# A CIN kernel: the contraction of 819 rows packed into six passes of 128 rows and one of 64 rows on two row tiles of TensorE

## Chip, cores and metric

One core of one Trainium2 chip. Times are device microseconds (us) of one execution; I quote the median of three or four, with the lowest and highest. Spans and everything else in a profile come from one profiled execution, which reads about 2 us shorter than its time. A run is told "slow" when it is over 1.5% above the fastest of the same kernel; ratios use fast runs only. Where kernels have slow runs among theirs, I compare their ratios to the kernel before: a difference of ratios times 860 us, the time of the kernel before.

## The reference

A compressed interaction network over x of shape (B, F, E) = (1024, 39, 64), fp32, with three layers of 64 outputs each and a final dot product:

```python
def _cin_layer(Xk, X0, W, b):
    Wr = W.reshape(O, Hk, Fdim)
    return jnp.einsum('bhe,bfe,ohf->boe', Xk, X0, Wr) + b[None, :, None]
Xk = X0
for W, b in ((W0, b0), (W1, b1), (W2, b2)):
    Xk = _cin_layer(Xk, X0, W, b)
    outs.append(Xk.sum(axis=-1))
return jnp.concatenate(outs, axis=-1) @ fc_w.T + fc_b
```

The kernel folds layers 2 and 3 into weights at the start. What is left per (b, e) is a contraction over the symmetric products x_i x_j, which with 39 linear rows are 819 rows, against 128 columns of weights.

## The kernel before

The batch is cut into 32 blocks of 2048 columns (32 samples of 64). Per block, x is loaded with one field per partition (`load`), stored twice below itself in DRAM (`store`), and copied back from there in rotated row orders (`roll`), so that the product of two copies yields 117 different pairs. Seven such products of 117 rows are made by VectorE and contracted by TensorE:

```python
def load(n, engine):                       # one transfer, issued by GpSimd
    engine.dma_start(xs[n]..., xv[:, n * BB : (n + 1) * BB, :])

def store(n):                              # 2 x 312 KB
    nc.sync.dma_start(xd[n][0:F], xs[n])
    nc.sync.dma_start(xd[n][F:FW], xs[n])

def roll(n):                               # 4 x 936 KB + 2 x 312 KB
    for i in range(4):
        nc.sync.dma_start(r[n][i], rows(xd[n], BASE[i], [(1, F), (STEP[i], NG)], BLK))
    nc.sync.dma_start(qt[0:K:NG], xd[n][LAST : LAST + F])
    nc.sync.dma_start(qt[1:K:NG], xd[n][0:F])
# ... cut: weights ...
def product(n, c):
    a, b = (r[n][PAIRS[c][0]], r[n][PAIRS[c][1]]) if c < len(PAIRS) else (r[n][0], q[n % 2])
    nc.vector.tensor_tensor(p, a, b, ALU.mult)          # 117 x 2048

def multiply(n, c, p):
    for m in range(BLK // MM):                          # 4 column groups of 512
        nc.tensor.matmul(po[n][m // 2][...], wa[:, c, :], p[:, bass.ts(m, MM)], ...)
# ... cut ...
for at, (n, c) in enumerate(steps):                     # 7 chunks a block
    if c == 0:
        roll(n + 1); store(n + 2); load(n + 3, nc.gpsimd)
    multiply(n, c, p.pop((n, c)))
    if c == 0:
        finish(n - 1); fields(n)
    p[steps[at + 4]] = product(*steps[at + 4])
```

One turn of the SP queue is thus: six copies for block n+1, then the store of block n+2. There are two sets of copies.

Of the kernel before, what the change touches and what calls it, by code (L numbers as in the profile page):

```python
# [33 lines left out]
F32 = mybir.dt.float32  # L37
AF = mybir.ActivationFunctionType
ALU = mybir.AluOpType
AX = mybir.AxisListType  # L40

B, F, E, H = 1024, 39, 64, 64
FH = F * H
NG = 3
K = NG * F
STEP = (0, 15, 9, 6)
BASE = (0, 3, 5, 20)
LAST = 11
PAIRS = ((0, 1), (0, 2), (1, 2), (0, 3), (1, 3), (2, 3))
NCHUNK = len(PAIRS) + 1  # L50
MM = 512
SUB = 1024
BLK = 2048
# [3 lines left out]
FW = 2 * F  # L57
# [3 lines left out]
    min(d % F, -d % F)  # L61
    for i, k in PAIRS
    for j in range(NG)
    for d in [(STEP[k] - STEP[i]) * j + BASE[k] - BASE[i]]
)
assert sorted(_dist + [LAST]) == list(range(1, F // 2 + 1))
assert max(2 * s + b for s, b in zip(STEP, BASE)) < F


def rows(t, first, steps, n):  # L70

    base = t[:]
    width = base.ap[-1][1] if len(base.ap) == 2 else n
    ap = [[s * width, k] for s, k in steps] + [[1, n]]
    return bass.AP(base.tensor, base.offset + first * width, ap)
# [3 lines left out]
def cin_kernel(ctx: ExitStack, tc: tile.TileContext, x, w0t, b0, w1, b1, w2, b2, fc_w, fc_b, out):  # L79
    nc = tc.nc  # L80
# [3 lines left out]
    const = ctx.enter_context(tc.tile_pool(name="const", bufs=1))  # L84
    dram = ctx.enter_context(tc.tile_pool(name="dram", bufs=1, space=DRAM))
    xds = ctx.enter_context(tc.tile_pool(name="xds", bufs=5, space=DRAM))
    stage = ctx.enter_context(tc.tile_pool(name="stage", bufs=4))
    rolls = ctx.enter_context(tc.tile_pool(name="rolls", bufs=2))
    prods = ctx.enter_context(tc.tile_pool(name="prods", bufs=4))
    psum = ctx.enter_context(tc.tile_pool(name="psum", bufs=4, space=PSUM))  # L90
    ctx.enter_context(tc.manual_schedule())

    xv = x.rearrange("b f e -> f b e")
    xs, xd, r = {}, {}, {}
# [10 lines left out]
        nc.sync.dma_start(xd[n][F:FW], xs[n])  # L105

    def roll(n):
        r[n] = [rolls.tile([K, BLK], F32, name=f"r{i}", tag=f"r{i}") for i in range(4)]
        for i in range(4):
            nc.sync.dma_start(r[n][i], rows(xd[n], BASE[i], [(1, F), (STEP[i], NG)], BLK))  # L110
        qt = q[n % 2]
        nc.sync.dma_start(qt[0:K:NG], xd[n][LAST : LAST + F])
        nc.sync.dma_start(qt[1:K:NG], xd[n][0:F])

    wa = const.tile([K, NCHUNK, 2 * H], F32, name="wa")
    wb = const.tile([K, NCHUNK, 2 * H], F32, name="wb")
    fc = const.tile([H, 3], F32, name="fc")
    fc2 = const.tile([H, 32], F32, name="fc2")
    v2 = const.tile([H, FX], F32, name="v2")
# [3 lines left out]
    wfin = const.tile([H + F, 1], F32, name="wfin")  # L123
    kfin = const.tile([1, 1], F32, name="kfin")

    q = [const.tile([K, BLK], F32, name=f"q{i}") for i in range(2)]

    wide0 = dram.tile([FW * FW, H], F32, name="wide0")
    wide0v = wide0.rearrange("(b a) h -> b (a h)", a=FW)
    wide = dram.tile([FX * FW, H], F32, name="wide")  # L130
# [3 lines left out]
    with prep as prep:  # L134

        w2s = prep.tile([H, FH], F32, name="w2s")
        w1s = prep.tile([H, FH], F32, name="w1s")
        nc.sync.dma_start(w2s, w2)
        nc.scalar.dma_start(fc, fc_w.rearrange("o (l h) -> h (o l)", h=H))
        nc.scalar.dma_start(w1s, w1)  # L140
        load(0, nc.sync)
        w0v = w0t.rearrange("b a h -> b (a h)")
        for i in range(2):
            for k in range(2):
                engine = nc.scalar if i else nc.gpsimd
                engine.dma_start(wide0v[i * F : (i + 1) * F, k * F * H : (k + 1) * F * H], w0v)
        nc.scalar.dma_start(bias[:, 0:1], b1.rearrange("(h o) -> h o", o=1))
        nc.scalar.dma_start(bias[:, 1:2], b2.rearrange("(h o) -> h o", o=1))
        nc.scalar.dma_start(b0s[H:128], b0.rearrange("(h o) -> h o", o=1))
        nc.scalar.dma_start(fcb, fc_b.rearrange("(p o) -> p o", o=1))  # L150
        for qt in q:
            nc.gpsimd.memset(qt, 1.0)  # L152
        store(0)
        roll(0)

        nc.vector.memset(wa[:, NCHUNK - 1, :], 0.0)
        nc.vector.memset(wb[:, NCHUNK - 1, :], 0.0)
        nc.vector.memset(wfin[0:H], 1.0)
        nc.vector.tensor_copy(fc2, fc[:, 2:3].to_broadcast([H, 32]))  # L159
        nc.vector.tensor_copy(v2[:, FW:FX], fc[:, 1:2].to_broadcast([H, 2]))  # L160


        n8 = 8 * F
        pv = psum.tile([128, 2, MM], F32, name="pv", tag="po")
        vrow = prep.tile([128, 2, n8], F32, name="vrow")
        for half in range(2):
            for t in range(4):
                g = 4 * half + t
                nc.tensor.matmul(  # L169
                    pv[32 * t : 32 * t + 32, half, 0:n8],  # L170
                    fc2,
                    w2s[:, g * n8 : (g + 1) * n8],
                    start=True,
                    stop=True,
                )
            nc.vector.tensor_copy(vrow[:, half], pv[:, half, 0:n8])  # L176
            nc.scalar.dma_start(v2[32 * half : 32 * half + 32, 0:F], vrow[0:128:32, half])
        nc.vector.tensor_copy(v2[:, F:FW], v2[:, 0:F])  # L178


        w1v = w1s.rearrange("o (h f) -> o f h", f=F)
        for g in range(5):
            f0, f1 = 8 * g, min(8 * g + 8, F)
            n = (f1 - f0) * H
            pt = psum.tile([128, SUB], F32, name="pt", tag="po")
            nc.tensor.matmul(pt[0:FX, :n], v2, w1v[:, f0:f1, :], start=True, stop=True)  # L186
            part = prep.tile([FX, MM], F32, name=f"part{g}")
            nc.vector.tensor_copy(part[:, :n], pt[0:FX, :n])  # L188
            for k in range(2):
                nc.scalar.dma_start(widev[:, (k * F + f0) * H : (k * F + f1) * H], part[:, :n])  # L190


    def gather(engine, dst, table, i, k, cols):

        first = BASE[k] * FW + BASE[i]
        steps = [(FW + 1, F), (STEP[k] * FW + STEP[i], NG)]
        engine.dma_start(dst[:, cols], rows(table, first, steps, H))  # L197

    def line(engine, dst, table, j, cols, first, step):
        engine.dma_start(dst[j:K:NG, NCHUNK - 1, cols], rows(table, first, [(step, F)], H))  # L200

    def gathers(engine, other, table, cols):
        for c, (i, k) in enumerate(PAIRS):
            gather(engine, wa[:, c], table, i, k, cols)
            gather(engine if c < 4 else other, wb[:, c], table, k, i, cols)
        line(engine, wa, table, 0, cols, LAST * FW, FW + 1)
        line(other, wb, table, 0, cols, LAST, FW + 1)
        line(engine, wa, table, 1, cols, 0, FW + 1)

    gathers(nc.gpsimd, nc.gpsimd, wide0, slice(H, 2 * H))  # L210
    load(1, nc.gpsimd)
    load(2, nc.gpsimd)
    gathers(nc.scalar, nc.sync, wide, slice(0, H))
    line(nc.sync, wa, wide, 2, slice(0, H), FW * FW, 1)
    store(1)


# [9 lines left out]
    po, g = {}, {}  # L227

    def product(n, c):
        a, b = (r[n][PAIRS[c][0]], r[n][PAIRS[c][1]]) if c < len(PAIRS) else (r[n][0], q[n % 2])  # L230
        p = prods.tile([K, BLK], F32, name="p", tag="p")
        nc.vector.tensor_tensor(p, a, b, ALU.mult)  # L232
        return p

    def multiply(n, c, p):
        if c == 0:
            po[n] = [psum.tile([128, SUB], F32, name="po", tag="po") for _ in range(BLK // SUB)]
        for m in range(BLK // MM):
            nc.tensor.matmul(  # L239
                po[n][m // 2][:, bass.ts(m % 2, MM)],  # L240
                wa[:, c, :],
                p[:, bass.ts(m, MM)],
                start=(c == 0),
                stop=(c == NCHUNK - 1),
            )

    def fields(n):
        g[n] = []
        for h in range(BLK // SUB):
            gt = work.tile([H + F, SUB], F32, name="g", tag="g")  # L250
            nc.scalar.copy(gt[H : H + F], xs[n][:, bass.ts(h, SUB)])  # L251
            g[n].append(gt)

    def finish(n):
# [15 lines left out]
    AHEAD = 4  # L270
    steps = [(n, c) for n in range(NBLK) for c in range(NCHUNK)]
    p = {s: product(*s) for s in steps[:AHEAD]}
    for at, (n, c) in enumerate(steps):
        if c == 0:
            if n + 1 < NBLK:
                roll(n + 1)
            if n + 2 < NBLK:
                store(n + 2)
            if n + 3 < NBLK:
                load(n + 3, nc.gpsimd)  # L280
        if n == 0:
            nc.vector.tensor_tensor(wa[:, c], wa[:, c], wb[:, c], ALU.add)  # L282
        multiply(n, c, p.pop((n, c)))
        if c == 0:
            if n > 0:
                finish(n - 1)
            fields(n)
        if at + AHEAD < len(steps):
            p[steps[at + AHEAD]] = product(*steps[at + AHEAD])
# [50 lines left out]
```

## Time and profile before

| | before |
|---|---|
| time, median of 4 runs | 861.1 us (858.1 to 863.2) |
| profiled span | 856.9 us |
| TensorE busy, one block in the steady stage | 24.03 us |
| moved by the SP queue (q1) per block: copies and store | 4992 KB in 8 transfers |

Four lines of the page of the kernel before: the span, the busy tenths of TensorE and of the 16 DMA engines in 40 slices, and the DMA queue of SP (packets, MB, and the time its packets took as a share of 16 engines' span).

```profile
span 856.9 us, 5040 instructions
...
PE   1446799999999999999999999999999999999996
...
DMA  6957645767666666665766666755776666565500
...
q1 hardware_dynamic: 25003, 164.63, 54.9%
```

TensorE is full in every slice after the start; the DMA engines are never full over a slice. A measure comes from the last line: 54.9% of 16 x 856.9 us, divided by 164.63 MB, is **45.7 us of engine time per MB**. A larger figure means that the same bytes keep the engines occupied for longer.

### The profile page before, as it was taken

Reading aid. Unit: us, or ns where it says so; the run is one execution under the profiler, and the core shown is the slowest. Engines: PE = TensorE matmul, PEld = TensorE weight load, DVE = VectorE, ACT = ScalarE, POOL = GpSimd, SP = SyncE. Lnnn points to the kernel's source line nnn. Section 1 sums busy time; section 2 is a strip of 40 time slices with the busy share of each in tenths; the row PEclk is TensorE's granted clock in tenths of the full one; section 3 lists DMA queues with packets and bytes.
Section 4 is the critical chain, followed back from the end, with each engine's and each line's share of the span. In section 5 each row is a group of like instructions: output and inputs, shape, how many; then the busy total and the mean of one; then the engine's idle time right before and its main releaser. Section 6 shows DMA issues by size and latency. Waiting matters only on the chain.

```text
span 856.9 us, 5040 instructions
## 1 busy us (share of the span) xinstructions
PE 794.1 (93%) x1828; PEld 346.0 (40%) x1828; DVE 664.1 (77%) x372; ACT 140.9 (16%) x133; POOL 44.0 (5%) x54
## 2 busy tenths in 40 slices
PE   1446799999999999999999999999999999999996
PEld 0112344444444444444444444444444444444442
DVE  0333488888888888888888888888888888888883
ACT  0010121122221111122222111122222111112221
POOL 4200000000000000000000000000000000000000
PEclk9998999999999999999999999999999999999998
DMA  6957645767666666665766666755776666565500
GB/s 187 255 142 241 241 177 197 230 210 218 254 240 234 213 233 218 221 215 211 248 242 251 196 237 195 244 215 216 237 242 251 215 225 232 193 210 204 187 0 1
DMA packets 32177, 179.41 MB, mean 209 GB/s; under 512 B 8487, under 2 KB 8686, under 8 KB 11901
## 3 DMA queue, kind: packets, MB, share of 16 engines
q1 hardware_dynamic: 25003, 164.63, 54.9%
q0 software_dynamic: 4080, 11.11, 5.8%
q10 hardware_dynamic: 3070, 3.35, 1.3%
q8 instruction: 14, 0.23, 0.1%
q14 instruction: 10, 0.08, 0.0%
HBM read 156.98 MB, written 23.61 MB: 211 GB/s over the span
## 4 chain that ended last, share of the span: by engine, by line
PE 89%; DMA 7%; issue 1%; DVE 1%; ACTq 1%; SPq 0%; ACT 0%; DVEq 0%
PE po L239 89%; DMA wide<-part 2%; DMA xs<-in_x 2%; DMA r<-xd 1%; DMA v<-vrow 1%; DMA xd<-xs 1%; ACTq L197 1%; DMA wa<-wide 0%; DVE g L262 0%; DVE sums L266 0%; PE pt L186 0%; PE py L295 0%; SPq L200 0%; DVE wa L282 0%; DMA q<-xd 0%
## 5 line engine op out<-in xcount | busy, mean ns | idle before, releaser
L239 PE MATMUL po<-p,wa 117*128 117x512 f32 x1792 | 778.8, 597 | 34.6 <-DVE wa L282 34.6
L232 DVE TENSOR_TENSOR p<-r,r 117x2048 f32<-117x2048 f32 x192 | 436.8, 2289 | 142.9 <-PE po L239 132.3
L239 PEld LDWEIGHTS po<-p,wa 117*128 117x128 f32 x1792 | 342.9, 192 | 469.9 <-issue 422.4
L258 ACT ACTIVATE x<-po,b0s 64x1024 f32<-64x1024 f32 x64 | 71.1, 1112 | 495.7 <-PE po L239 495.7
L251 ACT COPY g<-xs 39x1024 f32<-39x1024 f32 x64 | 66.7, 1043 | 156.4 <-DVE sums L266 156.4
L262 DVE SCALAR_TENSOR_TENSOR g<-po,fc,x 64x1024 f32<-64x1024 f32 x64 | 81.1, 1268 | 9.8 <-ACT x L258 9.8
L266 DVE TENSOR_REDUCE sums<-g 103x16 f32<-103x1024 f32 x64 | 78.1, 1220 | 2.2
L232 DVE TENSOR_TENSOR p<-r,q 117x2048 f32<-117x2048 f32 x32 | 73.1, 2284 | 3.8 <-issue 3.8
L98 POOL DMA_DIRECT2D xs<-in_x x31 | 30.1, 975 | 680.3 <-DMA xd<-xs 397.6
L186 PE MATMUL pt<-w1s,v 64*80 64x512 f32 (+1 forms) x10 | 9.5, 1109 | 13.7 <-DVE v L178 13.7
L222 ACT ACT_TABLE_LOAD x1 | 1.3, 1283 | 57.0 <-DMA wb<-wide 57.0
L186 PEld LDWEIGHTS pt<-w1s,v 64*80 64x80 f32 x10 | 2.2, 228 | 20.4 <-DVE v L178 14.7
L178 DVE COPY v<-v 64x39 f32<-64x39 f32 x1 | 0.2, 176 | 12.9 <-DMA v<-vrow 12.9
L169 PE MATMUL pv<-w2s,fc 64*32 64x312 f32 x16 | 2.5, 724 | 7.9 <-DVE fc L159 7.3
L188 DVE COPY part<-pt 80x512 f32<-80x512 f32 (+1 forms) x5 | 3.4, 673 | 6.8 <-PE pt L186 6.8
L295 PE MATMUL py<-sums,wfin 103*1 103x512 f32 x4 | 2.9, 814 | 3.7 <-DVE sums L266 3.7
L159 DVE COPY fc<-fc 64x32 f32<-64x32 f32 x1 | 0.2, 173 | 6.0 <-DMA fc<-in_fc_w 6.0
L197 POOL DMA_DIRECT2D wa<-wide x6 | 4.1, 686 | 9.5 <-DMA wide<-in_w0t 9.0
L197 POOL DMA_DIRECT2D wb<-wide x6 | 4.3, 716 | 2.2 <-DMA wb<-wide 2.2
L169 PEld LDWEIGHTS pv<-w2s,fc 64*32 64x32 f32 x16 | 0.4, 137 | 9.0 <-DVE fc L159 7.3
L152 POOL MEMSET q<- 117x2048 f32 x2 | 3.6, 1843 | 0.0
L176 DVE COPY vrow<-pv 128x312 f32<-128x312 f32 x2 | 1.0, 482 | 2.7 <-PE pv L169 2.7
(22 smaller groups left out, 9.1 us busy)
## 6 DMA issues: line engine op xcount, KB each, us to landing
r<-xd SPq DMA_DIRECT2D x128, 936.0 KB
xd<-xs SPq DMA_DIRECT2D x64, 312.0 KB
q<-xd SPq DMA_DIRECT2D x64, 312.0 KB
xs<-in_x POOLq DMA_DIRECT2D x31, 312.0 KB, 5.2
wide<-part ACTq DMA_DIRECT2D x8, 160.0 KB
wide<-in_w0t POOLq DMA_DIRECT2D x2, 380.2 KB, 9.7
wide<-in_w0t ACTq DMA_DIRECT2D x2, 380.2 KB
w2s<-in_w SPq DMA_DIRECT2D x1, 624.0 KB
```

What stands on the lines that cost most here:

```text
L98: engine.dma_start(xs[n].rearrange("p (b e) -> p b e", e=E), xv[:, n * BB : (n + 1) * BB, :])
L152: nc.gpsimd.memset(qt, 1.0)
L169: nc.tensor.matmul(pv[32 * t : 32 * t + 32, half, 0:n8], fc2, w2s[:, g * n8 : (g + 1) * n8], start=True, stop=True,)
L186: nc.tensor.matmul(pt[0:FX, :n], v2, w1v[:, f0:f1, :], start=True, stop=True)
L188: nc.vector.tensor_copy(part[:, :n], pt[0:FX, :n])
L197: engine.dma_start(dst[:, cols], rows(table, first, steps, H))
L232: nc.vector.tensor_tensor(p, a, b, ALU.mult)
L239: nc.tensor.matmul(po[n][m // 2][:, bass.ts(m % 2, MM)], wa[:, c, :], p[:, bass.ts(m, MM)], start=(c == 0), stop=(c == NCHUNK - 1),)
L251: nc.scalar.copy(gt[H : H + F], xs[n][:, bass.ts(h, SUB)])
L258: nc.scalar.activation(t, po[n][h][H:128, :], AF.Identity, bias=b0s[H:128])
L262: nc.vector.scalar_tensor_tensor(gt[0:H], po[n][h][0:H, :], fc[:, 0:1], x1[h], ALU.add, ALU.mult)
L266: nc.vector.tensor_reduce(sums[:, b_at : b_at + SB], gt.rearrange("p (b e) -> p b e", e=E), AX.X, ALU.add)
```

## The change

The intent: 117 rows of 128 leave a part of the array unused. The 819 rows are repacked into six chunks of 128 (117 + 11 rows) and one of 64 (62 of them used). The last is laid out so that half of its columns stand on partitions 0 to 63 and the other half on 64 to 127, and the two halves go through the two row tiles of TensorE (rows 0 to 63 and 64 to 127) at the same time. That should cut a block from seven passes to six and a half. The diff, cut to its core:

```diff
 def roll(n):
-    for i in range(4):
-        nc.sync.dma_start(r[n][i], rows(xd[n], BASE[i], ...))
-    nc.sync.dma_start(qt[0:K:NG], xd[n][LAST : LAST + F])
-    nc.sync.dma_start(qt[1:K:NG], xd[n][0:F])
+    for i in range(4):
+        t = r[n][i]
+        nc.sync.dma_start(t[0:K], rows(xd[n], BASE[i], ...))
+        if i:                                      # three of 11 rows, 88 KB
+            nc.sync.dma_start(t[K:128], xd[n][EXTRA[i] : EXTRA[i] + NX])
+    for t, pieces in (                             # ten into u and v, 24 to 224 KB
+        (ut[n % 2], ((0, 56, 0), (56, 62, 28))),
+        (vt[n % 2], ((0, F, 0), (45, 56, 34), (56, 62, F))),
+    ):
+        for p0, p1, first in pieces:
+            for h in range(2):
+                nc.sync.dma_start(t[h * HR + p0 : h * HR + p1],
+                    xd[n][first : first + p1 - p0, bass.ts(h, BLK // 2)])
 def product(n, c):
+    # c < 6: p = r_i * r_k, 128 x 2048;  c == 6: h = u * v, 128 x 1024
 def multiply(n, c, p):
     for m in range(BLK // MM):
+        w, at = slice(0, 128), bass.ts(m, MM)
+        if c == NPAIR:
+            h, m = m % 2, m // 2
+            w, at = slice(h * HR, (h + 1) * HR), bass.ts(m, MM)
+            m += h * (BLK // MM // 2)
         nc.tensor.matmul(po[n][m // 2][:, bass.ts(m % 2, MM)],
-            wa[:, c, :], p[:, bass.ts(m, MM)], ...)
+            wa[w, c, :], p[w, at], ...)
 def fields(n):
-    nc.scalar.copy(gt[H : H + F], xs[n][:, bass.ts(h, SUB)])
+    nc.scalar.copy(gt[H : H + F], ut[n % 2][h * HR : h * HR + F])
```

(The gathers that build the weights change with it. `HR` is 64.) The order of the turn stays: all copies, then the store. The copies of a block grow from 6 to 17 transfers and from 4368 to 4952 KB.

## The prediction

> **What bounds the kernel now.** I read the page first (chain, then groups), then the stages, then the waits of the DMA queue, because the change takes matmuls away and adds transfers. The chain that ended last and the groups:
>
> ```profile
> PE 89%; DMA 7%; issue 1%; DVE 1%; ACTq 1%; SPq 0%; ACT 0%; DVEq 0%
> ```
> ```profile
> L239 PE MATMUL po<-p,wa 117*128 117x512 f32 x1792 | 778.8, 597 | 34.6 <-DVE wa L282 34.6
> L232 DVE TENSOR_TENSOR p<-r,r 117x2048 f32<-117x2048 f32 x192 | 436.8, 2289 | 142.9 <-PE po L239 132.3
> L239 PEld LDWEIGHTS po<-p,wa 117*128 117x128 f32 x1792 | 342.9, 192 | 469.9 <-issue 422.4
> L262 DVE SCALAR_TENSOR_TENSOR g<-po,fc,x 64x1024 f32<-64x1024 f32 x64 | 81.1, 1268 | 9.8 <-ACT x L258 9.8
> L266 DVE TENSOR_REDUCE sums<-g 103x16 f32<-103x1024 f32 x64 | 78.1, 1220 | 2.2
> ```
>
> 89% of the chain is the main matmul. The program has 896 of them (32 blocks, 7 chunks, 4 column groups), the trace 1792: an fp32 matmul leaves two records, each with its own weight load. One lasts 597 ns but they overlap. The steady stage, the table by stretches:
>
> ```profile
> 400.00:500.00 100.00, 100.00 (x234) 44.27 (x233) 86.02 (x47) 17.24 (x16) 4.30 (x5) 1.00 0.64 221
> ```
>
> TensorE is busy all 100 us at full clock; 233 weight loads give 0.429 us per record, so a block of 7 x 4 x 2 = 56 records takes 24.03 us. VectorE's products wait for TensorE (132.3 us in all), never the other way after the start. Main matmuls run from 53.0 us, with pauses until block 0 ends at about 100.6; 31 blocks of 24.03 follow (745), then a tail of about 10. That is the 856.9 span.
>
> How near is the DMA side? The queue's own waits between 400 and 800 us, and one turn of the SP queue:
>
> ```profile
> SPq L110 <- DMA xd<-xs: 228.5, 16, 17.7
> SPq L110 <- DVE p L232: 63.4, 17, 6.5
> ```
> ```profile
> 404.66 3.62 SPq L110 DMA_DIRECT2D r<-xd  x4
> 408.32 0.74 SPq L112 DMA_DIRECT2D q<-xd  x1
> 409.10 0.74 SPq L113 DMA_DIRECT2D q<-xd  x1
> 409.89 0.54 SPq L104 DMA_DIRECT2D xd<-xs  x1
> 410.48 0.36 SPq L105 DMA_DIRECT2D xd<-xs  x1
> 428.69 3.43 SPq L110 DMA_DIRECT2D r<-xd  x4
> ```
>
> The turn is serial: the rotated copies of one block, then the store of the next, whose landing releases the next copies. Issuing takes 6.2 us; over 16.6 turns the wait for the store is 228.5/16.6 = 13.8 and the wait for the last product on the old tile 63.4/16.6 = 3.8. So a turn needs some 20 us of the 24: about 4 us to spare, no more.
>
> **What the Trainium skill says.** (1) "TensorEngine Tiling (Array Packing)", Key Properties: row tiles work independently, and changing the tiling mode drains the array. Independence shows in this trace, for column tiles: the 16 records of the small matmul pv (four column tiles) last 724 ns each and fill only 2.5 us of TensorE, and the table has four, then eight in flight:
>
> ```profile
> 7.50:7.80 0.30, 0.30 (x4) 0.04 (x4) 0.00 (x0) 0.00 (x0) 0.00 (x0) 1.00 0.98 375
> 7.90:8.00 0.10, 0.10 (x8) 0.00 (x0) 0.00 (x0) 0.00 (x0) 0.00 (x0) 1.00 3.25 917
> ```
> ```profile
> L169 PE MATMUL pv<-w2s,fc 64*32 64x312 f32 x16 | 2.5, 724 | 7.9 <-DVE fc L159 7.3
> ```
>
> No row tile pair and no drain inside a busy stream is in it. (2) The same page, Gotcha 1: row tiles must write different PSUM banks. The change keeps to this: its half chunk goes through column groups 0, 2, 1, 3, rows 0-63 and 64-127 in turn. (3) "TensorE: Matmul & The Clock Gate", Part 3: matmuls in different row groups run together, four row tiles at 3.07 times. Not in this trace. (4) "DMA: Bandwidth & Descriptors", Why a DMA increments its semaphore by 16: a transfer uses the largest number of engines up to 16 that divides its slowest dimension, on these queues the lowest-numbered ones. The trace agrees: 117 and 39 rows divide by 13, and while copies stream the DMA share stays at 0.77 to 0.89 (336 GB/s at 0.80), near 13/16 = 0.81.
>
> **The change, part by part.** The same 7 x 117 = 819 rows of the contraction go into six chunks of 128 rows and one of 64, of which two column groups run at a time.
>
> TensorE. Six chunks: 48 records x 0.429 = 20.6 us. Half chunk, ideal: 8 records two at a time = 1.72. Two mode changes per block: each should expose the end of the last matmul (597 - 429 = 168 ns) and perhaps a weight load (192 ns): 0.17 to 0.36 each, 0.5 us a block as an estimate. Sum 22.8, against 24.03: 1.2 saved per block. 128 rows for 117 cost nothing; a record streams 512 columns either way.
>
> VectorE. Six products of 2.29, one of half width (estimate from the two widths shown: about 1.2), and 2 x (1.27 + 1.22): 19.9 of 22.8 us. Not the bound. ACT's copies are unchanged.
>
> DMA. Per block the copies were 4 x 936 + 2 x 312 = 4368 KB; now 4 x 936 + 3 x 88 + 496 (u) + 448 (v) = 4952. With the store of 624: 4992 to 5576 KB, +12%. On the busiest engine: before 4 x 9 + 2 x 3 + 2 x 3 = 48 rows of 8 KB; now 36 + 3 x 1 + u (4 + 1) + v (3 + 1 + 1) + 6 = 55, +15%. Of the turn's 20 us some 18 are transfer: 20.2 to 20.7, with the fixed 2 us 22.2 to 22.7. There are 19 issues instead of 8, and the build makes most wait for the transfer eight places earlier; and the x load no longer waits for ACT, so it can fall on the start of the copies instead of the pause: 0 to 1.5 us more. So 22.2 to 24.2, against TensorE's 22.8: the two are about even. Copies are asked for a block ahead. From the start worked out below I estimate that the copies of block 2 begin some 10 us before TensorE would have to wait for them; spread over 30 blocks, a turn may be 0.35 us longer than TensorE's block before it is felt. A turn of 22.2 to 24.2 thus makes blocks of 22.8 to 23.9; I take 23.2.
>
> Start. SP has 11 more row copies in block 0 (at the 0.36 to 0.75 us that such issues take above, some 6 us) and six more gathers, and the first weight sum now waits for one of those, where SP's gathers were needed only later before: first main matmul at about 60 instead of 53. Against that, in block 0 TensorE pauses 2.6 us before each of six more chunks because the next weight sum stands behind a product that waits for a buffer; the half product has its own buffers, which lets VectorE get ahead: four of six pauses should go. Block 0 ends at about 95 instead of 100.6.
>
> Sum: 95 + 31 x 23.2 + 10 = 824 span. The median run is 6 us above the profiled span (862.8 against 856.9), so about 830.
>
> **Rivals.** (A) Row tiles don't overlap: the 8 records of the half chunk run in series, 8 x 0.429 = 3.43 us plus 0.5 of drains, so 24.5 a block and, with the same start and tail, about 870. Against it: the overlap of pv. For it: row tiles share the output columns, which column tiles don't. (B) DMA becomes the bound at 24.2 or more: 95 + 31 x 24 + 10 = 849, about 855. For it: 0.64 mean share, only 4 us spare, +12 to 15%, more and smaller transfers. Against: the spare is real in nearly every turn. (C) Both work, and drains cost little: 22.4 a block, 800 span, 805. (D) The start loses: gathers and extra rows queue so that block 0 ends at 110: +15 on any of these.
>
> **Range and chances.** C gives the low end; B with some of D the high. A I give 7%, B 20%, the rest lies between 805 and 840. Range 805 to 856. The 2% line is 845.5: faster 0.74, within 0.20, slower 0.06.
>
> **What would show it right or wrong.** Right: the table by stretches has about 241 weight loads per 100 us for 233 (a block still has 56 records, 48 + 8, but every 23.2 us); the half chunk's matmuls show two in flight and take under 2.4 us; no waits of products for r or u, v in the steady stage; the SP queue waits almost only for its transfers, little for products. Drains: gaps ahead of the half chunk and after it under 0.4 us. Wrong: the four half matmuls take 3.4 us (A); product waits for DMA of r appear and TensorE's busy share drops below 95% with blocks of 24 us (B); the first block ends after 105 us (D).

## The result, and the profile after

| | before | after |
|---|---|---|
| time, median of 4 runs | 861.1 us (858.1 to 863.2) | **966.1 us** (954.0 to 967.2) |
| ratio of fast runs | | **1.119** (95%: 1.109 to 1.129) |
| profiled span | 856.9 us | 963.3 us |
| mean granted clock | 0.99 | 0.96 |
| one block in the steady stage | 24.03 us | 27.4 us |
| engine time per MB, q1 | 45.7 us | 54.0 us |

A ratio here is always the mean time of one kernel's fast runs over that of the other's of the same rounds, so not quite the ratio of the medians. The kernel became 12% slower where I predicted 4% faster, far outside the range. The same lines of the page, of the kernel after, and its chain:

```profile
span 963.3 us, 5636 instructions
...
PE   1417999899879988889898799898979888898895
...
DMA  6947777777776776777777677777767777777650
...
q1 hardware_dynamic: 34773, 183.83, 64.4%
...
DMA 65%; DVE 14%; SPq 9%; issue 6%; PE 5%; ACTq 1%; ACT 0%; DVEq 0%; POOLq 0%
DMA r<-xd 35%; DMA u<-xd 18%; DMA xd<-xs 7%; DVE p L273 6%; SPq L128 5%; DVE g L312 5%; PE po L289 4%; DVE sums L316 4%; SPq L130 3%; DMA xs<-in_x 2%; DMA wide<-part 2%; DMA v<-vrow 1%; SPq L225 0%; SPq L137 0%; ACTq L225 0%
```

TensorE has holes all along and the DMA engines have lost their pauses (7 where there were 6 and 5). The chain that ended last, 89% matmul before, is 65% DMA, half of it the copies of r. And q1 moves 12% more with 18% more engine time for each MB (64.4% of 16 x 963.3 over 183.83 MB is 54.0).

A stretch of the table by stretches (stretch, length, busy us and records of PE, PEld, DVE, ACT, POOL; clock, DMA share, GB/s) has TensorE at 88.57 us of 100, with 207 weight loads where the kernel before had 233:

```profile
500.00:600.00 100.00, 88.57 (x208) 36.32 (x207) 68.81 (x39) 14.71 (x14) 2.90 (x3) 0.97 0.74 222
```

Yet TensorE's own part went as hoped. Its timeline over the half chunk of one block (start, duration, instructions):

```profile
585.20 5.36 PE L289 MATMUL po<-p,wa 128*128 128x512 f32 x11
590.48 1.99 PE L289 MATMUL po<-h,wa 64*128 64x512 f32 x8
592.40 4.13 PE L289 MATMUL po<-p,wa 128*128 128x512 f32 x9
```

The eight records of the half chunk take 1.92 us until the next chunk starts (592.40 - 590.48), where eight in series at 0.429 would take 3.43. (The mean granted clock is lower here, 0.96; but 14 of the 32 half chunks take 1.91 or 1.92 us, as in pe_only below at 0.99.) What starves TensorE is VectorE waiting for copies. The group of products, and one turn of the SP queue:

```profile
L273 DVE TENSOR_TENSOR p<-r,r 128x2048 f32<-128x2048 f32 x192 | 434.2, 2288 | 287.6 <-DMA r<-xd 221.4
```
```profile
519.94 2.39 SPq L128 DMA_DIRECT2D r<-xd  x2
...
525.28 0.52 SPq L130 DMA_DIRECT2D r<-xd  x1
525.92 8.39 SPq L137 DMA_DIRECT2D u<-xd  x4
537.89 7.26 SPq L137 DMA_DIRECT2D v<-xd  x6
545.25 0.30 SPq L121 DMA_DIRECT2D xd<-xs  x1
545.59 0.37 SPq L122 DMA_DIRECT2D xd<-xs  x1
549.76 2.37 SPq L128 DMA_DIRECT2D r<-xd  x2
```

In this turn the issues of u and v take from 525.92 to 545.15: they stand in the queue waiting for earlier transfers to land. Only then does the store of the next block get out, 25.3 us after the turn began (before, in the turn that the prediction quotes, after 5.2 us), and the next copies must wait for its landing: 549.76 is 3.8 us after its last issue ended, and SP issues nothing meanwhile. The kernel before shows a longer wait for the store, 13.8 us a turn in the prediction; but there the store is issued while the copies ahead of it are still under way, so the wait covers them as well. The waits of the queue over the span (us in total, times, longest):

```profile
SPq L137 <- DMA r<-xd: 388.1, 150, 6.9
SPq L128 <- DMA xd<-xs: 145.6, 64, 4.2
```

L137 is the line of u and v; L128, that of r, waits for the store, up to 4.2 us. The mean turn is shorter than this one: block 0 ends at 101.8 and block 31 at 951.95 in TensorE's timeline, so (951.95 - 101.76)/31 = 27.4 us.

### The profile page after: what moved, and what is told of

The parts are those of the page before. It is cut to its first block, busy times and chain, and to the rows that moved or that the text cites. A ratio compares the mean times of both kernels' runs of the same rounds, so it can differ in the third digit from the quotient of the medians.

```text
span 963.3 us, 5636 instructions
## 1 busy us (share of the span) xinstructions
PE 795.5 (83%) x1828; PEld 322.3 (33%) x1828; DVE 630.8 (65%) x372; ACT 137.7 (14%) x134; POOL 49.8 (5%) x62
## 3 DMA queue, kind: packets, MB, share of 16 engines
q1 hardware_dynamic: 34773, 183.83, 64.4%
## 4 chain that ended last, share of the span: by engine, by line
DMA 65%; DVE 14%; SPq 9%; issue 6%; PE 5%; ACTq 1%; ACT 0%; DVEq 0%; POOLq 0%
DMA r<-xd 35%; DMA u<-xd 18%; DMA xd<-xs 7%; DVE p L273 6%; SPq L128 5%; DVE g L312 5%; PE po L289 4%; DVE sums L316 4%; SPq L130 3%; DMA xs<-in_x 2%; DMA wide<-part 2%; DMA v<-vrow 1%; SPq L225 0%; SPq L137 0%; ACTq L225 0%
## 5 line engine op out<-in xcount | busy, mean ns | idle before, releaser
L289 PE MATMUL po<-p,wa 128*128 128x512 f32 x1536 | 719.5, 624 | 137.4 <-DVE p L273 97.4
L273 DVE TENSOR_TENSOR p<-r,r 128x2048 f32<-128x2048 f32 x192 | 434.2, 2288 | 287.6 <-DMA r<-xd 221.4
L289 PEld LDWEIGHTS po<-p,wa 128*128 128x128 f32 x1536 | 296.7, 198 | 558.6 <-issue 375.1
L301 ACT COPY g<-u 39x1024 f32<-39x1024 f32 x64 | 66.7, 1042 | 375.6 <-DVE sums L316 367.5
L308 ACT ACTIVATE x<-po,b0s 64x1024 f32<-64x1024 f32 x64 | 67.6, 1105 | 350.3 <-PE po L289 350.3
L289 PE MATMUL po<-h,wa 64*128 64x512 f32 x256 | 63.9, 615 | 0.0
L276 DVE TENSOR_TENSOR h<-u,v 128x1024 f32<-128x1024 f32 x32 | 39.0, 1220 | 0.0
L289 PEld LDWEIGHTS po<-h,wa 64*128 64x128 f32 x256 | 22.5, 186 | 39.2 <-issue 36.6
L225 POOL DMA_DIRECT2D wa<-wide x10 | 6.4, 642 | 9.5 <-DMA wide<-in_w0t 5.3
```

Source lines behind the costliest of these rows:

```text
L225: engine.dma_start(dst, rows(table, first, steps, H))
L273: nc.vector.tensor_tensor(p, r[n][PAIRS[c][0]], r[n][PAIRS[c][1]], ALU.mult)
L276: nc.vector.tensor_tensor(p, ut[n % 2], vt[n % 2], ALU.mult)
L289: nc.tensor.matmul(po[n][m // 2][:, bass.ts(m % 2, MM)], wa[w, c, :], p[w, at], start=(c == 0), stop=(c == NCHUNK - 1),)
L301: nc.scalar.copy(gt[H : H + F], ut[n % 2][h * HR : h * HR + F])
L308: nc.scalar.activation(t, po[n][h][H:128, :], AF.Identity, bias=b0s[H:128])
```

## The experiments

My theory after seeing this: TensorE's gain is real, and the turn of the SP queue has become the bound. Its rivals at that point: that the row tiles or the changes of mode cost TensorE time which the waits hide; that the late store alone is the cost; that the number of small transfers is; that their bytes, or where the bytes land, are. Labels in the texts stand for forms of these. None of them held alone: t_bal, gp, store_mid and mid_xs came out between the ranges expected from two of them, and swap above both. Edits are shown cut to their core. All kernels ran with three rounds beside the kernel before (858.5 to 861.7 us in those rounds). "Wrong" means that stale or partial data is multiplied, in the same shapes and at the same cost.

### Is TensorE's part right?

**pe_only**: the 13 small transfers are sent for blocks 0 and 1 only; wrong.

```diff
-            if i:
+            if i and n < 2:
...
-        for t, pieces in (
+        for t, pieces in () if n >= 2 else (
```

> The changed kernel, but the small transfers (three of 11 rows, ten for u and v) are made for blocks 0 and 1 only; wrong result on purpose, all engine instructions kept. Theory 1 (the transfers of a block's turn set the time): the turn loses 1208 KB and 13 of its 19 issues and falls below TensorE's block; TensorE's block is then 48 x 0.429 plus about 2.0 for the half chunk = 22.6 us, span about 102 + 31 x 22.6 + 10 = 812, no product waits for r in the steady stage. Theory 2 (row tiles or mode changes cost TensorE more than the trace shows, and the waits for transfers only follow): stays above 900.

Measured: 819.2 us (816.0 to 819.4), ratio 0.953 (0.948 to 0.957). A line of its table by stretches, and its half chunk in TensorE's timeline:

```profile
500.00:600.00 100.00, 100.00 (x247) 42.81 (x247) 84.88 (x48) 16.81 (x16) 3.87 (x4) 1.00 0.64 218
```
```profile
508.78 1.99 PE L289 MATMUL po<-h,wa 64*128 64x512 f32 x8
510.69 15.72 PE L289 MATMUL po<-p,wa 128*128 128x512 f32 x36
```

TensorE is full, with 247 records per 100 us: 56 x 100/247 = 22.7 us a block. The half chunk takes 510.69 - 508.78 = 1.91 us. In its timeline the half chunks of blocks 0 and 31 start at 99.91 and 804.07, so blocks are (804.07 - 99.91)/31 = 22.71 us apart. Streaming takes 48 x 0.429 for the six chunks and 8/2 x 0.429 for the half one, 22.31 in all; entering and leaving the half chunk thus costs the other 0.4. So the compute of the changed kernel, left alone, is 5% faster than before.

**pe_serial**: pe_only, but all four matmuls of the half chunk read rows 0 to 63, so one row tile; wrong.

```diff
-                w, at = slice(h * HR, (h + 1) * HR), bass.ts(m, MM)
+                w, at = slice(0, HR), bass.ts(m, MM)
```

> As pe_only, but all four half-chunk matmuls use rows 0 to 63 (wrong result on purpose), so nothing can overlap. If the two row tiles of the changed kernel run at the same time: 8 records in series, 3.43 us for 1.92, so about 1.5 us more per block, 48 us more in all than pe_only (about 860). If the row tiles were not overlapped in the first place: same time as pe_only.

Measured: 873.2 us (872.5 to 874.0), 1.016; that is 54 us more than pe_only, 1.7 us a block. Its timeline shows the half chunk at

```profile
515.06 3.70 PE L289 MATMUL po<-h,wa 64*128 64x512 f32 x8
```

3.63 us until the next chunk (518.69), for 1.91 in pe_only. (Its blocks are 24.42 us apart: 24.03 of streaming, and again 0.4.) The two row tiles do run side by side, and without that the change would lose even with free transfers.

### Is it the transfers, and which?

**before_dma**: the kernel before, with the list of transfers of the changed kernel (the extra rows go to tiles nobody reads; wrong).

```diff
+            if i and n >= 2:
+                nc.sync.dma_start(ex[32 * i : 32 * i + 11], xd[n][11 * i - 5 : 11 * i + 6])
+        # n >= 2: the ten transfers into ut, vt in place of the two into qt
```

> The kernel before with its own seven chunks and products, but from block 2 on with the transfers of the changed kernel in their order: the 11-row ones, u and v go to tiles that nobody reads, in place of the two for q (wrong result on purpose). Theory 1: transfers alone make the turn 27 to 28 us although TensorE has its old work: span 930 to 970. Theory 2 (the row tiles do it): stays at 857 to 870.

Measured: 969.5 us (967.3 to 978.5), 1.130. The list of transfers alone accounts for the loss; TensorE, row tiles and products are those of before.

**t_skew**: of the 13 small transfers only the three of 11 rows are kept; wrong.

```diff
-        for t, pieces in (
+        for t, pieces in () if n >= 2 else (
```

> The changed kernel with the three 11-row transfers of each block kept and the ten for u and v made for blocks 0 and 1 only (wrong result on purpose): 264 KB and three more issues than pe_only, one row more on 11 of the engines each. Theory 1b: 3 rows in 42, turn some 7% longer than in pe_only, still below 22.6: 817 to 825. Theory 1c: the engines come apart, packets of 8 KB get longer by 15% or more, span 830 to 900.

Measured: 820.3 us (820.1 to 820.8), 0.954. Beside pe_only these three transfers are free.

**t_bal**: pe_only plus six transfers of 39 rows each, 1248 KB a block (the changed kernel's 13 carry 1208), so that as many bytes come in fewer, evenly cut transfers; wrong.

```diff
+        if n >= 2:
+            for k in range(2):
+                nc.sync.dma_start(dead[64 * k : 64 * k + F], xd[n][9 * k : 9 * k + F])
+            for t in (ut[n % 2], vt[n % 2]):
+                for h in range(2):
+                    nc.sync.dma_start(t[h * HR : h * HR + F], xd[n][0:F, bass.ts(h, BLK // 2)])
```

> pe_only (817 us, blocks of 22.6) plus six transfers per block of 39 rows each, 1248 KB in all against the changed kernel's 1208, into a tile that nobody reads and into u and v (wrong result on purpose). All use the same 13 engines as the r copies, so each engine gets 54 rows of 8 KB per block, against at most 55 in the changed kernel. Theory 1b (bytes on the busiest engine fill the turn): as slow as the changed kernel, 940 to 970. Theory 1c (it is the uneven, small transfers of 6, 11 and 56 rows that set the engines apart and make the packets longer[...]): turn near 23, span 820 to 860.

Measured: 904.2 us (902.8 to 906.6), 1.052. The 85 us above pe_only are those of the bytes, evenly cut, and of a late store together: the two issues of the store still wait for transfers of r here, and leave 15.3 and 18.7 us into a turn (518.46, 533.79, 537.13). The changed kernel has some 60 us more than that.

### Order, issuer and number of the transfers

**swap**: the store of block n+2 is issued ahead of the copies of n+1; correct.

```diff
-            if n + 1 < NBLK:
-                roll(n + 1)
             if n + 2 < NBLK:
                 store(n + 2)
+            if n + 1 < NBLK:
+                roll(n + 1)
```

> The changed kernel with two lines exchanged: the store of block n+2 is issued before the copies of block n+1. Correct result. Theory 1a (the turn is long because it is serial: copies, then the store behind them, then its landing, then the next copies): the landing leaves the turn, which falls from 27.4 to the transfer alone, 21 to 24 us: span 810 to 860. Theory 1b (the bytes and packets alone fill the turn, engine share at its cap): 920 to 965.

Measured: 1065.8 us (1055 to 1081), 1.233: some 100 us worse, not better, with 62.1 us of engine time per MB. The waits for the store are gone, as intended, and the u and v issues wait 540 us in all for the copies of r instead of 388. My simple form of the theory, that an early store must help, fell here. Why the engines take 62 us per MB I could not settle.

**gp**: the 13 small transfers are issued by GpSimd in place of SP; correct.

```diff
-                    nc.sync.dma_start(
+                    nc.gpsimd.dma_start(
```

> The changed kernel with the 13 small transfers of each block issued by GpSimd instead of SP, correct result. The store then follows the four big copies at once, nothing waits eight places back[...]. Theory 1d (the queue of eight is the cost: the store is issued only when most of u and v have landed): turn falls by 4 us or more, span 820 to 850. Theory 1b (bytes): 930 or more. A new cost is possible: some 1 us of GpSimd per issue, 14 us a block.

Measured: 914.0 us (911.9 to 915.9), 1.062: some 50 us better than the change. In the profiles, 10 of these are the start (the half chunk of block 0 begins at 89.4 us, not at 99.5) and 1.3 us a turn the rest. SP now issues its four copies and the store at once (518.38 to 523.65 in one turn) and then waits for the store:

```profile
SPq L128 <- DMA xd<-xs: 670.2, 63, 23.6
```

The small issues still wait for earlier transfers, now in GpSimd's queue: 290 us in all for the store, 149 for transfers of u, 137 for those of r. So a good part of the loss is that the store stood behind waiting issues. But the turn is still longer than TensorE's 22.7 us: two x loads, one to a turn, are issued at 508.68 and 533.97, 25.3 us apart.

**fused**: the same bytes in six small transfers in place of 13: the three of 11 rows as one, u and v as whole 8 KB rows, with ScalarE moving one half of the columns to partitions 64 to 127; u and v are twice as wide, and the buffers of x go from four to two; correct.

```diff
+        nc.sync.dma_start(rt[n % 2][K:128, 1:4], rows(xd[n], EXTRA[1], [(1, NX), (LAST, 3)], BLK))
...
-                for h in range(2):
-                    nc.sync.dma_start(t[h * HR + p0 : ...], xd[n][first : ..., bass.ts(h, BLK // 2)])
+                nc.sync.dma_start(t[p0:p1], xd[n][first : first + p1 - p0])
...
+        for t in (ut[n % 2], vt[n % 2]):
+            nc.scalar.copy(t[HR : 2 * HR, 0 : BLK // 2], t[0:HR, BLK // 2 : BLK])
```

> The changed kernel, correct, with six small transfers instead of 13 and the same bytes: the three of 11 rows in one, u and v as whole rows of 8 KB (two and three transfers), their second half moved to partitions 64 up by ScalarE. Theory 1d (number of transfers): turn falls to 23 to 24.5, span 815 to 860. Theory 1b (bytes on the busiest engine, still 55 rows): 930 or more. Theory 1c (uneven transfers): in between, the packets stay longer than 400 ns.

Measured: 977.2 us (960 to 997), 1.125 from its two fast runs; the profile is of a slow run, so I take nothing fine from it. With half the transfers there is no gain, so their number alone is not the cost; but the two more copies of ScalarE and the fewer buffers of x changed with it (mid_thin below tests the number without them).

### The store, the x load and the bytes, one at a time

**store_mid**: the store goes between the copies of r with their extra rows, and the ten of u and v; correct.

```diff
             if n + 1 < NBLK:
                 roll(n + 1)
             if n + 2 < NBLK:
                 store(n + 2)
+            if n + 1 < NBLK:
+                small(n + 1)          # the ten transfers into u and v
```

> The changed kernel with the store of the next block issued between the 11 row copies and the ten of u and v, correct result. Theory 1d (exposed store: it is issued late, alone, and its 4 us to landing stand in the turn): those 4 us go beside u and v, turn 23.5, span 830 to 860. Theory 1e (transfers that flow on without a common pause let the engines drift apart and get slower, as in swap, where 1 MB cost 62 us of engine time against 54 in the changed kernel and 46 before): gain eaten, 920 to 1000.

Measured: 890.8 us (877.0 to 900.5), 1.028 (1.017 to 1.039). Beside the change (1.119) the place of two issues in the queue is worth (1.119 - 1.028) x 860 = 78 us, 2.5 us a turn. The queue's wait for the store, 145.6 us in the change, is nearly gone:

```profile
SPq L128 <- DMA xd<-xs: 10.4, 4, 4.2
```

**mid_xs**: store_mid, and the x load is issued by SP behind the store instead of by GpSimd. There it waited for transfers of v and so started just ahead of the next copies (at 504.79 in a turn whose copies start at 506.38). Correct.

```diff
-                load(n + 3, nc.gpsimd)
+                load(n + 3, nc.sync)
```

> As store_mid, and the load of x is issued on the SP queue behind the store instead of by GpSimd, so that it no longer runs into the row copies (in the changed kernel it does so in nearly every turn, in the kernel before hardly ever). If that collision costs 1 to 2 us a turn: 30 to 60 us below store_mid. If it doesn't matter: within 10 us of store_mid.

Measured: 867.5 us (857.7 to 875.2), 1.002 (0.994 to 1.010): 23 us less, 0.7 us a turn. With two fast runs in each of the two kernels, the intervals allow 11 to 35 us.

**xs_last**: the change, with only that one edit: the x load behind the store at the end of the turn; correct.

```diff
-                load(n + 3, nc.gpsimd)
+                load(n + 3, nc.sync)
```

> The changed kernel, correct, with one change: the load of x goes to the SP queue behind the store. If the collision of the x load with the row copies is a cause by itself: 20 to 50 us below the changed kernel's 966. If it only matters once the store is out of the turn's tail: within 10 us of 966, or worse, since the load then stands in the turn.

Measured: 999.4 us (998.6 to 1000.6), 1.162: 33 us more than the change by the medians. The x load is thus no cost of a fixed size: the same edit gained 23 us where the store stood early, and lost 33 here, where the load comes last in the turn. How it loses them is not shown: the queue waits less for the store than in the change (84.8 us for 145.6), and the engine time per MB is higher (56.6 us, x load included).

**mid_thin**: mid_xs with u and v a quarter as wide, the same 13 small transfers; wrong.

```diff
+                    w = BLK // 2 if n < 2 else BLK // 8
-                        t[h * HR + p0 : h * HR + p1],
+                        t[h * HR + p0 : h * HR + p1, 0:w],
```

> mid_xs with the same 13 small transfers, those of u and v a quarter as wide from block 2 on (236 KB instead of 944; wrong result on purpose). If the bytes cost the rest: TensorE's bound, 815 to 830. If the number of transfers does: 860 to 870.

Measured: 815.9 us (812.2 to 824.1), 0.950 (0.943 to 0.957), TensorE full:

```profile
500.00:600.00 100.00, 100.00 (x250) 42.70 (x249) 85.03 (x50) 19.95 (x19) 0.00 (x0) 1.00 0.68 227
```

With the store and the load placed well, the rest of the loss is bytes: the same number of transfers, 708 KB a block lighter, is at TensorE's bound. (That is more than the 584 KB which the change had added.)

**fused_mid**: mid_xs with the six small transfers of fused; correct.

```diff
-                for h in range(2):
-                    nc.sync.dma_start(t[h * HR + p0 : ...], xd[n][first : ..., bass.ts(h, BLK // 2)])
+                nc.sync.dma_start(t[p0:p1], xd[n][first : first + p1 - p0])
+        # and the three of 11 rows as one, ScalarE's two copies, as in fused
```

> mid_xs (867 us) with the same bytes in six small transfers instead of 13 (whole rows of 8 KB, second halves moved by ScalarE, as in fused), correct. If the number of transfers costs the rest (each waits for the one eight places back): 820 to 840. If the bytes do: 860 to 880.

Measured: 1023.0 us (982 to 1036), with one fast run of four, so no ratio. It missed badly what I expected. Its SP queue waits 193.8 us for products before its issues of u and v, which mid_xs does not (it waits 107.4 us there for ScalarE), and its DMA share is 0.82 to 0.83 in the stretches between 300 and 700 us at only 200 to 207 GB/s. I take from it only that fewer transfers of the same bytes, made in this way, do not help. Why they hurt is open.

### A version that keeps the gain

**diag_mid**: the diagonal rows of u and v (x_i times x_i, straight copies of x) are copied by ScalarE from the tile that the x load has filled, which takes u and v from 944 to 376 KB a block; the three of 11 rows go as one; the store stands before u and v; the x load is GpSimd's, as in the change. With its 640 KB of small transfers, q1 moves 5008 KB a block for the 4992 of before. Correct.

```diff
     def small(n):
-            (ut[n % 2], ((0, 56, 0), (56, 62, 28))),
-            (vt[n % 2], ((0, F, 0), (45, 56, 34), (56, 62, F))),
+            (ut[n % 2], ((32, 56, 32), (56, 62, 28))),
+            (vt[n % 2], ((45, 56, 34), (56, 62, F))),
+    def diagonal(n):
+        for t, k in ((ut[n % 2], 32), (vt[n % 2], F)):
+            for h in range(2):
+                nc.scalar.copy(t[h * HR : h * HR + k], xs[n][0:k, bass.ts(h, BLK // 2)])
```

> A version meant to beat both, correct: row tiles as in the changed kernel, but the diagonal rows of u and v are copied by ScalarE from the x tile that is in SBUF already (four copies of about 1.04 us a block), which leaves 376 KB for u and v instead of 944; the three 11-row transfers are one; the store comes before u and v, and x is loaded as in the kernel before. 5008 KB a turn against 4992 before, 50 rows on the busiest engine against 48. Theory 1 (bytes and landing make the turn): turn 21 to 22.6, TensorE is the bound again, span 815 to 835. Theory 1e (drift): 850 to 930.

Measured: **817.9 us** (812.4 to 823.3), ratio **0.950** (0.944 to 0.957). It beats both kernels and is as fast as pe_only, with a correct result. (In the profiles this is in part the start: blocks are 23.04 us apart, 22.71 in pe_only, but the half chunk of block 0 begins 5.9 us earlier. The profile is of the slowest of the four runs.) A stretch and a turn of the SP queue:

```profile
500.00:600.00 100.00, 100.00 (x247) 42.93 (x246) 85.25 (x49) 38.72 (x37) 4.83 (x5) 1.00 0.78 246
```
```profile
516.23 0.29 SPq L126 DMA_DIRECT2D r<-xd  x1
516.57 3.32 SPq L130 DMA_DIRECT2D r<-xd  x4
519.99 0.49 SPq L121 DMA_DIRECT2D xd<-xs  x1
520.53 0.35 SPq L122 DMA_DIRECT2D xd<-xs  x1
520.98 6.62 SPq L139 DMA_DIRECT2D u<-xd  x4
531.89 5.08 SPq L139 DMA_DIRECT2D v<-xd  x4
537.26 0.29 SPq L126 DMA_DIRECT2D r<-xd  x1
```

The store leaves 3.8 us after the turn's start, lands beside the u and v traffic, and the next copies follow the last v at once (536.97 to 537.26). ScalarE pays: 39 us busy per 100 for 17, which it has to spare.

**diag_last**: diag_mid with the store moved back behind u and v; correct.

```diff
-            if n + 2 < NBLK:
-                store(n + 2)
             if n + 1 < NBLK:
                 small(n + 1)
+            if n + 2 < NBLK:
+                store(n + 2)
```

> As diag_mid with the store after u and v, the order of the changed kernel. Theory 1d: turn longer than in diag_mid by the exposed store, 2 to 4 us: 840 to 900. Theory 1e: the common pause keeps the engines together, same as diag_mid or faster.

Measured: 901.0 us (897.0 to 908.7), 1.050. One edit of order, 83 us; same bytes, same transfers. In the profiles about 6 of these are the start (the half chunk of block 0 begins at 100.3 us, not at 94.0), which leaves some 2.5 us a turn. Its queue waits again for the store:

```profile
SPq L126 <- DMA xd<-xs: 120.4, 32, 4.2
```

which in diag_mid is

```profile
SPq L126 <- DMA xd<-xs: 7.8, 2, 4.2
```

As few bytes as before are thus not enough: with the store last and behind eight small issues they give 901 us.

**diag_xs**: diag_mid with the x load on SP behind the store; correct.

```diff
             if n + 2 < NBLK:
                 store(n + 2)
+            if n + 3 < NBLK:
+                load(n + 3, nc.sync)
             if n + 1 < NBLK:
                 small(n + 1)
-            if n + 3 < NBLK:
-                load(n + 3, nc.gpsimd)
```

> diag_mid (818 us) with the load of x on the SP queue behind the store. It is at TensorE's bound already (pe_only 817), so 812 to 820; if the load in the turn makes the turn longer than 22.6, 825 or more.

Measured: 821.0 us (816.0 to 829.9), 0.953: the same as diag_mid. At TensorE's bound the place of the load no longer matters.

## Why the prediction was wrong

The prediction's steps, in its order.

1. **TensorE bounds the kernel before, 24.03 us a block: right.** Nothing in the runs speaks against it.
2. **The half chunk in 1.72 us plus 0.5 of mode changes, 22.8 us a block: right.** pe_only has 22.71. What is left beside the streaming, 0.4 us a block, is near the 0.5 that I put down for two mode changes (half of it within the 1.91 us, which alone would show only 0.2). That the changes of mode are its cause is my reading; pe_serial, which also enters and leaves 64-row matmuls, has the same 0.4. As the prediction assumed, 128 rows cost no more than 117: the weight loads inside pe_only's full chunks follow each other by 0.43 us. Rival A (no overlap) is refuted by pe_serial.
3. **VectorE is not the bound: right.** In the steady stage of pe_only it is 85% busy and TensorE is full; in the changed kernel it is idle because it waits for the copies of r.
4. **The turn of the DMA queue, "22.2 to 24.2 ... the two are about even": this is the step that failed.** It measured 27.4 us. The rule behind it was right (TensorE waits once the turn is longer than its block), the size was not. The step had two terms, and both were too small:
   - *"with the fixed 2 us"*: I took the exposed landing of the store as in the kernel before, where the store leaves 5.2 us after the turn's start and lands in the wake of the copies. I saw that most small transfers wait for one eight places earlier, and counted it among "0 to 1.5 us more". What I missed is who stands behind them in the same queue: the store, which thereby left 25.3 us into the turn and landed alone, 3.8 us after its issue in the turn shown, and which the next turn waits for. diag_mid against diag_last prices that place in the queue at 83 us, some 2.5 us a turn; the change against store_mid at 78 us, 2.5 a turn.
   - *"Of the turn's 20 us some 18 are transfer: 20.2 to 20.7"*: I scaled bytes and rows of the kernel before at an unchanged rate. Engine time per MB rose from 45.7 to 54.0 us, 18%. At that rate 20.2 to 20.7 become some 24 (an estimate, 20.45 x 54.0/45.7 = 24.2). So the bytes weighed more than their 12 to 15%. With the store placed well, what bytes still cost is mid_xs against mid_thin: (1.002 - 0.950) x 860 = 45 us, 1.4 us a turn, for 708 KB a block. The x load is another 0.7 us a turn in the one setting where I could take it out (store_mid to mid_xs), inside my 0 to 1.5, but xs_last shows that it is not a sum that can be added in any order.

   Taken in the order store, load, bytes, the steps from the change to TensorE's bound are 78, 23 and 45 us, in all (1.119 - 0.950) x 860 = 145 us or 4.7 us a turn, which is the difference between 27.4 and the 22.7 of pe_only (some 7 of the 145 us are the start: the half chunk of block 0 begins at 99.5 us in the change, at 92.5 in mid_thin). By the intervals each part is good to about 9 to 13 us either way, and in another order the parts would differ.

   The count of 55 rows rests on point (4) of the skill, and the agreement that I read there is weak: one of the five shares behind it, 0.89, lies above 13/16, so the trace does not show how many engines a copy uses.
5. **The spread of a turn over a head start, "0.35 us longer before it is felt":** of no use, as the turn was over 4 us too long; it went into the 23.2 and so made the wrong term look harmless.
6. **The start, block 0 at about 95: half right.** TensorE's pauses before weight sums went from seven to three, as hoped, but the first main matmul came at 68.6 us, not at 60, so block 0 ended at 101.8. It is 7 us of the 136 that I was off. (The 6 us from span to median were 3: 966.1 against 963.3.) Rival D's mechanism was there, at half its size.

Of the rivals, B (the DMA as the bound) had the right direction and 20%, but I sized it at 24 us from the same wrong terms. I gave weight to "the spare is real in nearly every turn", without asking whether the spare would survive a new order of events in the queue. Of my signs for "wrong", that of B came true to the letter: the product waits for r are 221 us, and TensorE's busy share is 86 to 89% in the stretches between 300 and 700.

**What stays open.** Why the same MB occupies the engines for 54 us in the change, 62 in swap and 65 in fused_mid (a slow run), but 46 in pe_only and 51 in diag_mid. It is not the number of transfers alone (mid_thin has all 13 and 48.4; its q1, like fused_mid's, carries the x load too), not the short 11-row ones (t_skew 47.9), and not the bytes alone (diag_last 54.1 and diag_mid 51.0 move the same). Order and overlap of reads, stores and loads have a part in it; no run separated which.

## What to carry to other kernels

When a change adds transfers to a queue, look for what stands behind them in the same queue: an issue that waits for an earlier transfer holds back everything after it (here the store, which stood behind u and v from 525.92 to 545.25), and if the next round waits for that, the wait is exposed in full. Place the transfer on which the next round depends ahead of the ones that only have to arrive in time. Don't scale a queue's time by bytes at its old rate when its spare is a few microseconds; test the list of transfers alone first (as before_dma did), since it needs none of the new compute.

## What the Trainium skill lacked or had wrong

- "TensorEngine Tiling (Array Packing)", Key Properties, says that tiles run in parallel and that a change of tiling mode drains the array; for the first the page has only a theoretical "Up to 2×", for the second no time. Here four fp32 matmuls of 64 rows and 512 columns (two records each) take 1.91 us on two row tiles for 3.63 on one (pe_only, pe_serial), and going into the half chunk and out of it costs about 0.4 us a block in both, beside the streaming.
- "DMA: Bandwidth & Descriptors", Issuing engines are not separate DMA queues, says that issuing from several engines saves only the sequencer's time, "usually small relative to the DMA itself". Here moving 13 issues to GpSimd gained 1.3 us of a turn of 27.4 (gp): in the change they wait for earlier transfers, 388.1 us in all for those of r, and hold back the store behind them. That section does not speak of such waits.
- No page says that engine time per MB depends on the order of the same transfers: it was 51.0 us in diag_mid and 54.1 in diag_last, 54.0 in the change and 62.1 in swap, for 45.7 in the kernel before. The runs do not show why.
